# A conditional residual kernel: tile 0 and W's first half issued by two engines, with a new order of tasks

## The chip, the cores and the metric

The kernel runs on 1 core of one Trainium2 chip. The metric is the device time of one execution in microseconds. Before the change the median of 3 runs is 108.7 us (108.12 to 109.39).

## What is computed

```python
def _L0_cond_ref(hidden0, hidden1, x, W, b):
    hidden = jnp.concatenate([hidden0, hidden1], axis=-1)
    x_mean = jnp.mean(x, axis=1, keepdims=True)
    ones_L = jnp.ones((1, L, 1), dtype=x.dtype)
    fused = jnp.concatenate([x, x_mean * ones_L, hidden[:, None, :] * ones_L], axis=-1)
    relation = jax.nn.relu(jnp.einsum('bld,do->blo', fused, W) + b)
    return relation
x = x + _L0_cond_ref(cond_512, cond_512, x, L0_cond_W, L0_cond_b)
```

x is (4, 1024, 512), cond_512 (4, 256), W (1536, 512), b (512), all float32. The first 512 rows of W meet x itself. The next 512 meet the mean of x over a batch row, and the last 512 meet the condition, so those two give one bias vector per batch row. The output is x + relu(x @ W[:512] + bias of the row).

## The kernel before, in words

The 4096 rows of x make 32 **tiles** of 128 rows, 8 to a batch row. A product in float32 is split into high and low parts: a value's `hi` is its float32r rounding and `lo` is the rest, and a tile's result is the sum over four chunks j of 128 columns of hi x w_hi, lo x w_hi and hi x w_lo. That is 12 matmuls for a tile, and 384 for all (the last tile is done in two halves of 256 columns, so it has 24 short ones, and the trace has 396).

x is read twice. Task `Z` loads it in 512-byte rows into one of three `z` buffers, so that VectorE's 32 x 32 transposes (task `T`, L228) give x transposed; ScalarE rounds that to `hi` and sums it for the mean (`h`, L234); VectorE or GpSimd subtracts to get `lo` (`l`, L240). Tiles are taken in **units**: tile 0, tile 1, tiles 2 and 3, and then four at a time. Units are loaded in four quarters of 32 partitions (`Z4.2` is quarter 2 of unit 4). Task `X` loads x a second time, two tiles at once, for the last addition.

W's first 512 rows come in two halves, W0 (chunks j = 0 and 1) and W1 (j = 2 and 3), each in four quarters. `wh` rounds a chunk to w_hi (L204 on ScalarE, L206 on VectorE) and `wl` subtracts to w_lo (L210). `M` loads W's second 512 rows (tile w_mean), `V` the last 512, `C` the condition and `B` b.

**The bias of a batch row r** is a chain in PSUM bank `acc`: ScalarE copies the condition's part there (`as`, L279), VectorE adds four products of w_mean with the row's means (`m`, L284), ScalarE and VectorE fold and split it (`f` L292, `fa` L296, `vh` L300, `vl` L304), one matmul with ones spreads it (`pb`, L308), and ScalarE copies it out (`bc`, L312). The means of row r need all of that row's `h` (`to`, L272 to L275, on GpSimd).

A tile's output leaves PSUM in one of three ways. Tiles 0 to 11 are parked by ScalarE (`K`, L397), then GpSimd adds the bias (`b`, L401), ScalarE takes the relu (`r`, L409) and GpSimd adds x (`F`, L413). Tiles 12 to 17 are parked by VectorE with the bias added (L405). For tiles 18 to 31 ScalarE first puts the bias into the bank (`P`, L384 and L364) and VectorE does relu and addition in one instruction (`F`, L388 and L368). `S` stores a tile. There are five PSUM banks for products; tile t uses bank t mod 5.

**What sets the order** is one table, ORDER (L21 to L49): names of tasks in the order in which they are written, with `@d`, `@a`, `@p` for VectorE, ScalarE and GpSimd (or, for a load, `@a` for ScalarE's DMA queue instead of SyncE's). Each engine does its own tasks strictly in that order, and waits are set by a scheduling layer from the data. DMAs, in the order of the table, take eight completion semaphores in turn, so a DMA waits until the one eight places ahead of it has landed. `fill` is a matmul on zeros (L128) that gives TensorE something to do before the first product.

Before the change `one` is put through a relu (L123), with which ScalarE's function table is loaded, ahead of all tasks. After all tasks, 8 matmuls into `acc` (L427) are issued whose result nobody reads.

Of the kernel before, what the change touches and what calls it, by code (L numbers as in the profile page):

```python
# [18 lines left out]


ORDER = """  # L21
W0.0@a W0.2@a W0.1@a W0.3@a Z0.0 Z0.2 Z0.1 Z0.3 Z1.0 Z1.2 Z1.1 Z1.3 wh0l@d wh0r@a wh1@a W1.0 W1.2 W1.1 W1.3
wl0r@d wl0l@d T0.0 T0.1 h0.0 wl1@d h0.1 l0.0@p fill fill fill fill fill fill fill fill fill fill fill p0.0.0
p0.0.2 Z2.0 Z2.2 Z2.1 Z2.3 p0.1.0 T1.0 l0.1@p T1.1 p0.1.2 h1.0 T0.2 p0.0.1 T0.3 h1.1 p0.1.1 T1.3 p1.0.0 h0.3
l1.0@d p1.0.2 l1.1@d h1.3 l0.3@p p1.1.0 Z3.0 Z3.2 Z3.1 Z3.3 wh3@d h0.2 p1.0.1 p1.1.2 wh2@d l0.2@p p0.3.1 T1.2
p0.3.0 wl3@d l1.3@p p0.2.0 h1.2 p0.2.1 l1.2@p p1.3.0 wl2@d p1.3.2 C p1.2.0 T2.2 V p1.1.1 p0.2.2 T2.0 h2.2 B
p1.2.1 p1.3.1 h2.0 Z4.0 Z4.2 Z4.1 Z4.3 l2.2@d p1.2.2 p0.3.2 T2.3 p2.2 l2.0@d h2.3 p2.0 l2.3@d T2.1 p2.3 h2.1
l2.1@d p3.0 Z5.0 Z5.2 Z5.1 Z5.3 p3.1 T3.3 p2.1 T3.2 h3.3 t2 p3.2 T3.0 h3.2 l3.3@p p3.3 K1@a l3.2@d h3.0 t3
ac0@p t1 p6.2 T3.1 K2@a l3.0@d p4.2 M0 M2 M1 M3 h3.1 t0 p4.3 l3.1@p g0.0 p6.0 K0@a K3@a p6.3 ac1@p p6.1 d0.0
g0.1 p7.0 T4.3 Z6.0 Z6.2 Z6.1 Z6.3 p4.0 T4.1 h4.3 p4.1 T4.0 K6@a l4.3@p T4.2 h4.1 p5.3 h4.2 p7.3 l4.1@p h4.0  # L30
p7.1 K4@a l4.0@d d0.1 p8.3 g1.0 T5.1 p5.2 Z7.0 Z7.2 Z7.1 Z7.3 l4.2@d to0 as0 p5.0 d1.0 T5.3 h5.1 p11.3 T5.2
p5.1 T5.0 l5.1@p p8.2 h5.0 m0.0 p8.1 g1.1 X5.0 m0.1 g2.0 p9.0 d1.1 Z8.0 Z8.2 Z8.1 Z8.3 m0.2 h5.3 p11.0 h5.2
m0.3 l5.3@p p9.3 K5@a l5.0@d p11.2 f0 d2.0 g2.1 p8.0 fa0 p9.2 l5.2@d K8@a d2.1 T6.1 p7.2 vh0 p10.1 vl0 X0.0
K7@a T6.2 p13.3 h6.1 X0.1 T6.3 p10.3 l6.1@p T6.0 pb0 X1.0 p9.1 bc0@a to1 p10.0 as1 b2@p X4.0 K9@a p11.1 m1.0
g3.0 p13.0 b0@p m1.1 Z9.0 Z9.2 Z9.1 Z9.3 h6.3 p10.2 m1.2 g3.1 b1@p p14.0 h6.0 m1.3 p12.0 l6.0@d f1 l6.3@p
p12.1 T7.1 K10@a p12.3 K11@a fa1 b5@p p14.1 T7.0 vh1 X4.1 h7.1 p12.2 vl1 b3@p h6.2 p15.0 T7.3 h7.0 l6.2@d pb1
l7.1@p p14.2 h7.3 T7.2 p16.3 bc1@a l7.0@d h7.2 p13.2 T8.0 as2 to2 p16.2 l7.3@p r0 m2.0 p15.1 r1 m2.1 r2 F0
p14.3 m2.2 p15.3 F1 m2.3 p15.2 K12@d f2 p13.1 d3.0 S1 fa2 p16.0 X5.1 T8.1 S0 vh2 p17.2 b4@p X3.0 h8.0 vl2
p17.1 r5 l8.0@d pb2 F2 p16.1 K13@d bc2@a p17.3 T8.3 P18 F5 p17.0 K14@d r3 h8.1 l7.2@d p18.3 P19 K17@d l8.1@p
p18.2 T8.2 P22 p18.0 T9.0 F3 h8.2 p19.1 r12 l8.2@d p22.3 h9.0 d3.1 T9.1 p22.1 h8.3 T9.2 p18.1 r4 K15@d l8.3@p  # L40
h9.1 p22.2 F18 P20 p19.0 F4 T9.3 P23 p19.3 h9.2 p20.1 S4 K16@d h9.3 S18 p23.1 as3 to3 X2.0 b6@p P21 S2 p23.0
m3.0 S3 p19.2 m3.1 X2.1 b10@p r6 X3.1 p21.3 m3.2 S5 p20.3 X1.1 l9.3@p m3.3 p23.2 l9.2@d f3 p20.2 b7@p fa3
p22.0 F19 vh3 b9@p p20.0 vl3 p21.1 F20 F12 pb3 F22 p21.2 S20 bc3@a X6.1 l9.0@d p21.0 b8@p P27 r7 p23.3 P24
l9.1@p p27.0 F23 P25 p27.2 r8 F21 F6 p27.1 S21 P26 S22 p27.3 F7 S12 p25.2 S6 F27 S19 p25.3 P31r S7 r9 p24.2
X6.0 r10 p31.3r P28 p25.1 F10 r16 p31.2r p31.1r F9 p31.0r S10 p26.2 X7.1 p25.0 b11@p p24.1 F25 p24.0 F8 S25
P30 p26.0 S27 r17 F31r X7.0 r13 p26.1 S8 r11 p28.1 r14 F11 p26.3 p24.3 F26 F17 p28.3 F24 S26 P31l p30.1 S9 F16
P29 S24 p28.2 r15 S17 S11 p30.3 F14 S23 p29.2 S16 F15 p28.0 S14 p30.0 F28 F13 p31.3l S28 p30.2 S31r p29.0 S15
F30 p29.3 S30 p29.1 S13 p31.0l F29 p31.1l p31.2l S29 F31l S31l
""".split()  # L49


# [1 line left out]
def kernel(  # L53
# [66 lines left out]
    nc.vector.memset(one, 1.0)  # L120
# [298 lines left out]
    for name in ORDER:  # L419
# [3 lines left out]
        name, _, engine = name.partition("@")  # L423
        tasks.pop(name)(engine)

    for m, c in ((P, 0), (96, 0), (96, 0), (66, 0), (66, 0), (P, 1), (P, 1), (P, 0)):
        nc.tensor.matmul(acc[:m], lhsT=his[0][:, c : c + m], rhs=w_hi[:, 1], start=True, stop=True)  # L427


# [25 lines left out]
```

## Time and profile before

| | |
|---|---|
| median of 3 runs | 108.7 us |
| the profiled execution, its time | 109.66 us |
| its span, first to last instruction | 107.9 us |
| TensorE busy (PE) | 97.9 us, 91% of the span |
| GpSimd busy (POOL) | 74.8 us, 69% |
| VectorE busy (DVE) | 67.3 us, 62% |
| ScalarE busy (ACT) | 62.0 us, 57% |
| DMA moved | 28.41 MB, mean 263 GB/s |

The profile is one execution. A timeline row gives the start and the busy time in us, the engine, the line and the instruction; behind it in brackets stands how long the engine was idle before it and what ended that. SPq and ACTq are SyncE's and ScalarE's sequencers issuing DMAs; PEld is TensorE loading weights. Matmuls overlap, so the distance of their starts says more than their durations.

### The profile page before, as it was taken

What the parts mean: (1) busy time and instruction counts of PE and PEld (TensorE: products, weight loads), DVE (VectorE), ACT (ScalarE), POOL (GpSimd) and SP (SyncE); (2) the same over time, 40 slices, a digit from 0 to 9 for tenths busy, and PEclk for the clock granted to TensorE, in tenths of its full rate; (3) what the DMA queues carried; (4) which work ended last, traced back from release to release, by engine and by line L of the source; (5) the groups of instructions that cost most, each with busy time, mean ns of one, the idle gap of its engine ahead of it and who ended that gap; (6) DMA issues with size and microseconds to landing.
All of it is one profiled execution on the core that took longest, in us unless ns stands there. A gap on an engine that the chain in (4) does not pass through costs nothing.

```text
span 107.9 us, 1436 instructions
## 1 busy us (share of the span) xinstructions
PE 97.9 (91%) x419; PEld 77.1 (71%) x419; DVE 67.3 (62%) x121; ACT 62.0 (57%) x153; POOL 74.8 (69%) x75
## 2 busy tenths in 40 slices
PE   6913999999999999999999999999999899979960
...
DMA  2878699999999999999999995099999984499995
GB/s 84 186 255 242 167 222 351 249 221 223 231 242 231 221 227 237 226 219 260 387 286 215 258 378 232 21 301 362 343 407 406 374 262 147 178 276 406 403 405 191
DMA packets 27633, 28.41 MB, mean 263 GB/s; under 512 B 1637, under 2 KB 18281, under 8 KB 27626
## 3 DMA queue, kind: packets, MB, share of 16 engines
...
## 4 chain that ended last, share of the span: by engine, by line
DMA 26%; DVE 16%; POOL 15%; ACT 12%; SPq 10%; PE 8%; issue 7%; ACTq 0%; DVEq 0%; POOLq 0%
DMA x<-in_x_dram 13%; SPq L142 10%; DMA w_mean<-in_L_cond_W_dram 8%; POOL x L413 7%; PE po L330 6%; DVE acc L284 5%; ACT hi L234 5%; POOL lo L240 5%; DVE xT L228 3%; DMA z<-in_x_dram 3%; POOL cond L266 2%; DVE w_lo L210 2%; ACT o L409 2%; DMA x<-in_L_cond_W_dram 2%; DVE lo L240 2%
## 5 line engine op out<-in xcount | busy, mean ns | idle before, releaser
L330 PE MATMUL po<-w_hi,hi 128*128 128x512 f32 (+1 forms) x132 | 51.7, 393 | 5.0 <-ACT hi L234 3.9
L330 PE MATMUL po<-w_lo,hi 128*128 128x512 f32 (+1 forms) x132 | 51.1, 388 | 0.0
L330 PE MATMUL po<-w_hi,lo 128*128 128x512 f32 (+1 forms) x132 | 50.7, 387 | 0.0
L330 PEld LDWEIGHTS po<-w_hi,hi 128*128 128x128 f32 x132 | 25.3, 192 | 11.9 <-ACT hi L234 4.8
L240 POOL TENSOR_TENSOR lo<-xT,hi 128x512 fp32r<-128x512 f32 (+1 forms) x20 | 22.2, 1118 | 16.4 <-ACT hi L234 16.4
L330 PEld LDWEIGHTS po<-w_lo,hi 128*128 128x128 f32 x132 | 25.2, 191 | 5.0
L330 PEld LDWEIGHTS po<-w_hi,lo 128*128 128x128 f32 x132 | 25.2, 191 | 5.0
L413 POOL TENSOR_TENSOR x<-o,x 128x512 f32<-128x512 f32 x18 | 22.9, 1295 | 6.8 <-ACT o L409 6.1
L388 DVE SCALAR_TENSOR_TENSOR x<-po,x 128x512 f32<-128x512 f32 x13 | 8.7, 686 | 16.5 <-DMA x<-in_x_dram 8.1
L401 POOL TENSOR_TENSOR o<-o,bias 128x512 f32<-128x512 f32 x12 | 15.3, 1296 | 0.0
L234 ACT ACTIVATE hi<-xT 128x512 fp32r<-128x512 f32 (+2 forms) x24 | 11.9, 498 | 5.1 <-DVE xT L228 5.1
L228 DVE STREAM_TRANSPOSE xT<-z 128x512 f32<-128x512 f32 (+2 forms) x24 | 12.5, 539 | 3.7 <-DMA z<-in_x_dram 2.4
L284 DVE SCALAR_TENSOR_TENSOR acc<-w_mean,tot,acc 128x512 f32<-128x512 f32 x16 | 12.1, 756 | 2.5 <-DMA w_mean<-in_L_cond_W_dram 1.3
L240 DVE TENSOR_TENSOR lo<-px,hi 128x512 fp32r<-128x512 f32 (+1 forms) x16 | 10.3, 642 | 2.2 <-ACT hi L234 2.1
L384 ACT ACTIVATE po<-bias 128x512 f32<-128x512 f32 x13 | 7.5, 589 | 6.8 <-DVE x L388 6.5
L409 ACT ACTIVATE o<-o 128x512 f32<-128x512 f32 x18 | 10.6, 619 | 0.9 <-POOL o L401 0.9
L234 ACT ACTIVATE hi<-px 128x512 fp32r<-128x512 f32 (+1 forms) x16 | 9.0, 560 | 2.6 <-DVE px L228 2.5
L228 DVE STREAM_TRANSPOSE px<-z 128x512 f32<-128x512 f32 (+1 forms) x16 | 10.3, 660 | 0.1
L397 ACT ACTIVATE o<-po 128x512 f32<-128x512 f32 x12 | 6.9, 589 | 0.3 <-PE po L330 0.2
L266 POOL TENSOR_TENSOR cond<-cond,term 128x512 f32<-128x512 f32 x4 | 5.2, 1302 | 1.9 <-ACT term L262 1.9
L262 ACT ACTIVATE term<-wc,cT 128x512 f32<-128x512 f32 x8 | 5.6, 718 | 1.0 <-POOL wc L256 0.9
L128 PE MATMUL acc<-warm 128*128 128x512 bf16 x11 | 4.9, 632 | 1.0 <-DVE one L120 1.0
...
## 6 DMA issues: line engine op xcount, KB each, us to landing
...
out_dram<-x SPq DMA_DIRECT2D x31, 256.0 KB, 3.6
z<-in_x_dram SPq DMA_DIRECT2D x28, 256.0 KB, 8.4
...
w_mean<-in_L_cond_W_dram SPq DMA_DIRECT2D x4, 256.0 KB, 8.5
z<-in_x_dram SPq DMA_DIRECT2D x8, 64.0 KB, 2.5
x<-in_L_cond_W_dram ACTq DMA_DIRECT2D x4, 128.0 KB, 2.8
x<-in_L_cond_W_dram SPq DMA_DIRECT2D x4, 128.0 KB, 3.4
```

The costliest lines, as they stand in the source:

```text
L142: (nc.scalar if e == "a" else nc.sync).dma_start(**kw)
L228: nc.vector.transpose(xT.rearrange("p (n t) -> p n t", t=Q), zs[u % Z_BUFS][:, : n * NQ, j * Q : (j + 1) * Q])
L234: nc.scalar.activation(his[buf][:, col : col + m], xT, AF.Copy, accum_out=sums[:, r, j, s : s + 1])
L240: nc_of[e].tensor_tensor(los[buf][:, col : col + m], xT, his[buf][:, col : col + m].bitcast(F32), ALU.subtract)
L266: nc.gpsimd.tensor_tensor(conds[r % 2], conds[r % 2] if k else b_sb, terms[k], ALU.add)
L284: nc.vector.scalar_tensor_tensor(acc, w_mean[:, j, :], tot[:, r, j : j + 1], acc, ALU.mult, ALU.add)
L330: nc.tensor.matmul(v, lhsT=a[:, col : col + P], rhs=m, start=WAYS[t] != "I" and key not in done, stop=done.count(key) == 3 * J - 1, skip_g ...
L384: nc.scalar.activation(bank(t), biases[r], AF.Copy)
L388: nc.vector.scalar_tensor_tensor(x_tile(t), bank(t), 0.0, x_tile(t), ALU.max, ALU.add)
L401: nc_of[e].tensor_tensor(o, o, biases[r], ALU.add)
L409: nc.scalar.activation(o, o, AF.Relu)
L413: nc.gpsimd.tensor_tensor(x_tile(t), o, x_tile(t), ALU.add)
```

## The change

ORDER is another table. In it, ScalarE's queue issues quarters 2 and 3 of tile 0's z and quarters 2 and 3 of W0, and SyncE's queue the other quarters of these and everything else; before, ScalarE's queue issued all of W0 and nothing else. The relu on `one` becomes a task, placed behind those four issues. There are 12 fills at the start and not 11, and one more fill after the first two tiles. w_hi and w_lo of W0 are made in half chunks that are spread over more engines: `wl0r` goes to GpSimd, and several `wh` and `l` tasks change engines. The 8 matmuls at the end are gone. The rest of the table holds the same tasks in another order.

```diff
 ORDER = """
-W0.0@a W0.2@a W0.1@a W0.3@a Z0.0 Z0.2 Z0.1 Z0.3 Z1.0 Z1.2 Z1.1 Z1.3 wh0l@d wh0r@a wh1@a W1.0 W1.2 W1.1 W1.3
+Z0.2@a Z0.3@a Z0.0 Z0.1 W0.0 W0.1 W0.2@a W0.3@a relu Z1.2 Z1.3 Z1.0 Z1.1 T0.0 W1.2 W1.3 T0.1 h0.0 T0.2 h0.1
...
     nc.vector.memset(sums, 0.0)
-    nc.scalar.activation(one, one, AF.Relu)
     nc.gpsimd.memset(b_sb, 0.0)
...
+    @task("relu")
+    def _(e):
+        nc.scalar.activation(one, one, AF.Relu)
...
-    for m, c in ((P, 0), (96, 0), (96, 0), (66, 0), (66, 0), (P, 1), (P, 1), (P, 0)):
-        nc.tensor.matmul(acc[:m], lhsT=his[0][:, c : c + m], rhs=w_hi[:, 1], start=True, stop=True)
```

What that moves is seen in the built programs. Lines after L123 have other numbers there: L142 of the kernel before is L141 of the changed one, L228 is L231, L284 is L287, and so on.

**ScalarE at the start of the program**, before the change. x_63 is the buffer that takes W's first half, DMAHW1 and DMAHW4 are semaphores of earlier loads:

```order
L123 ACT_TABLE_LOAD
L123 ACTIVATE one<-one 128x1 [waits DVE_49]
L142 DMA x_63<-in_L_cond_W_dram 32x2x512 x2
L142 DMA x_63<-in_L_cond_W_dram 32x2x512 [waits DMAHW1_49]
L142 DMA x_63<-in_L_cond_W_dram 32x2x512 [waits DMAHW4_49]
```

and after it, where z_69 is tile 0's z:

```order
L141 DMA z_69<-in_x_dram 32x4x128 x2
L141 DMA x_63<-in_L_cond_W_dram 32x2x512 x2
L158 ACT_TABLE_LOAD
L158 ACTIVATE one<-one 128x1 [waits DVE_49]
L237 ACTIVATE hi_75,sums<-xT_120 128x128 [waits DVE_49] x2
```

All four loads of the changed kernel stand ahead of the table load and wait for nothing. Before, two of the four quarters of W0 waited for a landing.

**SyncE's loads in the first third of the program**, before. z_69, z_70 and z_71 are the three z buffers, x_64 takes W's last 512 rows:

```order
L142 DMA z_69<-in_x_dram 32x16x128 x4
L142 DMA bias_118<-in_cond_dram 4x256
L142 DMA x_64<-in_L_cond_W_dram 128x2x1024
L142 DMA b_sb<-in_L_cond_b_dram 1x512
L142 DMA z_70<-in_x_dram 32x16x128 x4
L142 DMA z_71<-in_x_dram 32x16x128 x4
L142 DMA w_mean<-in_L_cond_W_dram 32x4x512 x4
L142 DMA z_69<-in_x_dram 32x16x128 x4
```

and after it:

```order
L141 DMA z_69<-in_x_dram 32x16x128 x4
L141 DMA bias_118<-in_cond_dram 4x256
L141 DMA x_64<-in_L_cond_W_dram 128x2x1024
L141 DMA z_70<-in_x_dram 32x16x128 x4
L141 DMA b_sb<-in_L_cond_b_dram 1x512
L141 DMA w_mean<-in_L_cond_W_dram 32x4x512 x4
L141 DMA z_71<-in_x_dram 32x16x128 x4
L141 DMA z_69<-in_x_dram 32x16x128 x4
```

The load of w_mean has gone ahead of unit 5 (the z_71 there); unit 6, the last row, has the same loads ahead of it as before.

**VectorE around the bias chain of batch row 1**, before. The transposes of z_69 are unit 6, those of z_70 unit 7:

```order
L228 STREAM_TRANSPOSE px_142<-z_69 128x512 [waits DVE_49]
L228 STREAM_TRANSPOSE xT_121<-z_69 128x512 [waits Pool_49]
L228 STREAM_TRANSPOSE px_141<-z_69 128x512
L284 SCALAR_TENSOR_TENSOR acc<-w_mean,tot,acc 128x512 [waits DVE_49,Activation_49,Pool_49]
L284 SCALAR_TENSOR_TENSOR acc<-w_mean,tot,acc 128x512 [waits DVE_49] x3
L240 TENSOR_TENSOR lo_91<-px_141,hi_77 128x512 [waits PE_49,Activation_49]
L228 STREAM_TRANSPOSE xT_120<-z_70 128x512 [waits DMAHW5_49,DMAHW6_49,DMAHW4_49,DMAHW3_49]
L296 TENSOR_TENSOR acc<-acc,fold 64x512 [waits Activation_49]
L228 STREAM_TRANSPOSE px_141<-z_70 128x512 [waits DVE_49]
L304 TENSOR_TENSOR v_acc<-acc,v_acc 64x512 [waits PE_49,Activation_49]
```

and after it:

```order
L231 STREAM_TRANSPOSE px_141<-z_69 128x512
L287 SCALAR_TENSOR_TENSOR acc<-w_mean,tot,acc 128x512 [waits Activation_49,Pool_49]
L231 STREAM_TRANSPOSE xT_121<-z_69 128x512
L231 STREAM_TRANSPOSE xT_120<-z_69 128x512 [waits Pool_49]
L287 SCALAR_TENSOR_TENSOR acc<-w_mean,tot,acc 128x512 [waits DVE_49]
L243 TENSOR_TENSOR lo_91<-px_141,hi_77 128x512 [waits PE_49,Activation_49]
L287 SCALAR_TENSOR_TENSOR acc<-w_mean,tot,acc 128x512 [waits DVE_49]
L243 TENSOR_TENSOR lo_93<-px_142,hi_79 128x512 [waits PE_49,Activation_49]
L287 SCALAR_TENSOR_TENSOR acc<-w_mean,tot,acc 128x512 [waits DVE_49]
L231 STREAM_TRANSPOSE px_141<-z_70 128x512 [waits DMAHW5_49,DMAHW6_49,DMAHW4_49,DMAHW3_49]
L231 STREAM_TRANSPOSE xT_121<-z_70 128x512 [waits Pool_49]
L299 TENSOR_TENSOR acc<-acc,fold 64x512 [waits Activation_49]
```

The four additions of row 1's means, which stood together, now have transposes and subtractions of unit 6 between them, and two transposes of unit 7 stand ahead of the fold (L299) instead of one.

More of the change, by code (lines that the diff above doesn't have):

```diff
@@ L21 @@
 ORDER = """
-W0.0@a W0.2@a W0.1@a W0.3@a Z0.0 Z0.2 Z0.1 Z0.3 Z1.0 Z1.2 Z1.1 Z1.3 wh0l@d wh0r@a wh1@a W1.0 W1.2 W1.1 W1.3
[L23 to L46, printed above, removed]
@@ L47 @@
-P29 S24 p28.2 r15 S17 S11 p30.3 F14 S23 p29.2 S16 F15 p28.0 S14 p30.0 F28 F13 p31.3l S28 p30.2 S31r p29.0 S15
-F30 p29.3 S30 p29.1 S13 p31.0l F29 p31.1l p31.2l S29 F31l S31l
+Z0.2@a Z0.3@a Z0.0 Z0.1 W0.0 W0.1 W0.2@a W0.3@a relu Z1.2 Z1.3 Z1.0 Z1.1 T0.0 W1.2 W1.3 T0.1 h0.0 T0.2 h0.1
+l0.0@d wh1l@a wh1r@d W1.0 W1.1 l0.1@p wh0r@d wh0l@a wl1r@d fill fill fill fill fill fill fill fill fill fill
+fill fill p0.1.0 h0.2 wl0r@p wl0l@d p0.0.0 Z2.0 Z2.1 T1.1 p0.0.1 T1.0 wl1l@d p0.1.1 h1.0 Z2.2 Z2.3 T0.3 p0.0.2
@@ new lines @@
+h1.1 T1.2 p0.1.2 T1.3 p1.0.2 l1.1@p h1.2 l1.0@d p1.0.0 Z3.0 Z3.1 p1.1.0 l0.2@p p1.0.1 wh3@a wh2@d p1.1.1
+l1.2@p p1.1.2 Z3.2 Z3.3 wl2@d h1.3 p0.2.1 h0.3 p1.3.0 l1.3@d p1.2.0 l0.3@p p1.2.1 C wl3@d p1.2.2 V p0.2.0
+p1.3.1 Z4.0 Z4.1 p1.3.2 T2.3 p0.3.0 p0.3.1 T2.2 h2.3 p0.2.2 Z4.2 Z4.3 p0.3.2 K1@a l2.3@d T2.0 h2.2 fill p3.3
+T2.1 h2.0 l2.2@p p2.3 h2.1 l2.0@d l2.1@d B p2.2 p3.2 M0 M1 p3.1 T3.0 p3.0 T3.3 h3.0 p2.0 M2 M3 h3.3 l3.0@d
+p2.1 K0@a l3.3@p t2 t1 p6.0 T3.2 K3@a p4.0 T3.1 K2@a ac0@p h3.2 p4.3 h3.1 l3.2@d p7.3 Z5.2 Z5.3 l3.1@p t0 t3
```

19 lines of the change are left out of this document (added).

## The prediction

> **What bounds the kernel now.** I began with the page's first two parts: which engine is full, and when.
>
> ```profile
> PE 97.9 (91%) x419; PEld 77.1 (71%) x419; DVE 67.3 (62%) x121; ACT 62.0 (57%) x153; POOL 74.8 (69%) x75
> PE   6913999999999999999999999999999899979960
> DMA  2878699999999999999999995099999984499995
> ```
>
> TensorE is full from the fifth slice almost to the end; the low ones are the third and fourth, 5 to 11 us into the program. Next, what it waits for:
>
> ```profile
> PE po L330 <- ACT hi L234: 3.9, 1, 3.9
> PE po L330 <- ACT po L384: 0.5, 1, 0.5
> PE po L330 <- ACT po L364: 0.5, 1, 0.5
> ```
>
> One wait of 3.9 us stands ahead of the first product; the next are of 0.5. So the kernel is a stream of 396 products whose start is late, and whose end sets the end of the program. The stream itself, from the timeline of TensorE:
>
> ```profile
> 9.73 0.79 PE L330 MATMUL po<-w_hi,hi 128*128 128x512 f32 x1 [3.89 <-ACT hi L234]
> 11.18 0.63 PE L330 MATMUL po<-w_lo,hi 128*128 128x512 f32 x1
> 12.46 0.63 PE L330 MATMUL po<-w_hi,hi 128*128 128x512 f32 x1
> 15.71 0.39 PE L330 MATMUL po<-w_hi,lo 128*128 128x512 f32 x1
> 17.07 0.39 PE L330 MATMUL po<-w_hi,hi 128*128 128x512 f32 x1
> 102.14 0.28 PE L330 MATMUL po<-w_lo,hi 128*128 128x256 f32 x1
> 102.26 2.02 PE L427 MATMUL acc<-w_hi,hi 128*128 128x512 f32 x8
> ```
>
> Between 11.18 and 12.46 lie three products, 0.427 us each; between 15.71 and 17.07 six, 0.227 us each. TensorE thus starts at half rate and is at full rate well before 15.71. The product at 17.07 is number 25, the first that needs tile 2 or 3. From the last product (102.26) to the end of the span it is 5.6 us: an addition, a store and its landing.
>
> **The start, and what the change does to it.** The issues and what waits for them:
>
> ```profile
> 0.72 4.14 SPq L142 DMA_DIRECT2D z<-in_x_dram  x8
> 0.98 0.86 ACTq L142 DMA_DIRECT2D x<-in_L_cond_W_dram  x2
> 0.97 4.88 PE L128 MATMUL acc<-warm 128*128 128x512 bf16 x11 [0.97 <-DVE one L120]
> 3.78 1.27 ACTq L142 DMA_DIRECT2D x<-in_L_cond_W_dram  x2
> 4.90 1.85 SPq L142 DMA_DIRECT2D x<-in_L_cond_W_dram  x4
> 7.81 0.93 ACT L204 ACTIVATE w_hi<-x 128x256 fp32r<-128x256 f32 x2 [5.60 <-DMA x<-in_L_cond_W_dram]
> z<-in_x_dram SPq DMA_DIRECT2D x8, 64.0 KB, 2.5
> x<-in_L_cond_W_dram ACTq DMA_DIRECT2D x4, 128.0 KB, 2.8
> x<-in_L_cond_W_dram SPq DMA_DIRECT2D x4, 128.0 KB, 3.4
> ```
>
> ScalarE issues two quarters of W0 by 1.84 and then nothing until 3.78: the third waits for a quarter of tile 0's z (in the built order, DMAHW1), the fourth for another. So W0 is whole only at 7.8, and VectorE, which has w_hi and w_lo ahead of tile 0's transposes, brings the first product to 9.73.
>
> In the changed program the first eight loads are tile 0 and W0, four on each queue, and none waits. At 0.43 us an issue (0.86 for two) the last pair is issued from about 2.0. With 2.8 us to landing W0 is whole at 4.9, against 7.8. Tile 0 lands near 3.8 and is transposed and rounded while W0 is under way. The first product then needs half a chunk of w_hi, 0.4 us: 5.4. But 12 fills stand ahead of it, and at 4.88 us for 11 (0.43 apart) they end at 6.1. So the **first product is at 6.1**, 3.6 us sooner.
>
> Not all of that is kept, since after 12 products chunks 2 and 3 are wanted. SyncE issues W1 behind unit 1's four quarters, and those wait for tile 0's landing (3.3 to 3.8); that makes 5.1 to 6.9 where 4.90 to 6.75 was. W1 lands 3.4 us after its last issue began, at 9.9; w_hi takes 0.5 us, so product 13 is at about 10.5. The 12 products before it need 12 x 0.427 = 5.1 us at half rate and 2.7 at full, and have 4.4: they fit or nearly do. Another 12 x 0.227 = 2.7 us later, product 25 can start at 13.3 where it was 17.07: **-3.7 us**. Bounds: -2.0 if W1 is a microsecond later and the stream still slow, -4.0 if W1 is a little sooner. The new fill costs 0.2 and falls into a wait for unit 2. The table load now runs beside transfers; even a microsecond later it holds `h0` and then w_hi, and the wait for W1 covers that.
>
> [...]
>
> **The middle.** Being 3.7 us ahead only helps if every later wait has that much room. The tightest is the bias chain, at the three `pb` matmuls:
>
> ```profile
> 40.27 0.69 DVE L228 STREAM_TRANSPOSE xT<-z 128x512 f32<-128x512 f32 x1
> 43.97 3.13 DVE L284 SCALAR_TENSOR_TENSOR acc<-w_mean,tot,acc 128x512 f32<-128x512 f32 x4 [0.30 <-POOL tot L275]
> 49.55 0.69 DVE L304 TENSOR_TENSOR v_acc<-acc,v_acc 64x512 fp32r<-64x512 f32 x1
> 50.61 0.39 PE L308 MATMUL acc<-v_acc,ones 128*128 128x512 f32 x1
> 58.77 0.39 PE L330 MATMUL po<-w_lo,hi 128*128 128x512 f32 x1
> 59.55 0.50 PE L308 MATMUL acc<-v_acc,ones 128*128 128x512 f32 x1 [0.39 <-DVE v_acc L304]
> ```
>
> For batch row 1 v_acc is done at 50.24 and used at 50.61: 0.37 us of room. For row 2 TensorE waits, and 0.78 us instead of 0.23 lie between two starts. So a stream 3.7 us ahead runs into `pb1` unless that chain comes sooner too. In front of it stand transfers:
>
> ```profile
> 30.28 1.96 SPq L142 DMA_DIRECT2D z<-in_x_dram  x1
> 25.98 9.17 DMA w_mean<-in_L_cond_W_dram
> z<-in_x_dram SPq DMA_DIRECT2D x28, 256.0 KB, 8.4
> ```
>
> w_mean lands at 35.15 before. In the changed order it is ahead of unit 5's 1 MB and should land near 29, so row 0's bias is some 5 us sooner. Unit 6, whose last quarter is issued at 30.28 and with 8.4 us lands near 38.7 to 39.8, has as many bytes ahead of it as before, and the DMA engines are nearly full from slice 6 on; it gains at most the 1 us by which unit 3 can start sooner. And from unit 6's first transpose to v_acc VectorE now has, in order, 8 transposes, 4 additions of means, 2 subtractions, the fold and the split:
>
> ```profile
> L228 DVE STREAM_TRANSPOSE px<-z 128x512 f32<-128x512 f32 x14 | 9.4, 693 | 0.1
> L284 DVE SCALAR_TENSOR_TENSOR acc<-w_mean,tot,acc 128x512 f32<-128x512 f32 x16 | 12.1, 756 | 2.5 <-DMA w_mean<-in_L_cond_W_dram 1.3 <-POOL tot L275 0.8
> L240 DVE TENSOR_TENSOR lo<-px,hi 128x512 fp32r<-128x512 f32 x14 | 9.5, 676 | 1.6 <-ACT hi L234 1.6
> ```
>
> 8 x 0.69 + 4 x 0.76 + 2 x 0.68 + 2 x 0.69 = 11.3 us, less some 0.8 since neighbours overlap a little: 10.5. From a first transpose at 38.8 to 39.9 (40.27 before, as VectorE was busy) v_acc is done at 49.3 to 50.4; I take 49.9. Two more products stand ahead of `pb1` than before, so it would be reached at 48; it **waits about 2 us**, and of the lead 1.0 us is left (0.3 to 1.6). From there to `pb2` the chain (copy of the bias, four additions, fold, split and two parkings) needs about as long as the products between, so row 2's wait of 0.55 is partly kept: lead 1.3. `pb3` has room before and after. **The lead after the middle is 1.2 us** (0.3 to 3.5, the upper end where unit 6 is early and the chain doesn't bind).
>
> **The tail.** Here TensorE waits twice more:
>
> ```profile
> 83.07 0.39 PE L330 MATMUL po<-w_lo,hi 128*128 128x512 f32 x1
> 84.00 0.39 PE L330 MATMUL po<-w_hi,hi 128*128 128x256 f32 x1 [0.55 <-ACT po L364]
> 95.91 0.50 PE L330 MATMUL po<-w_hi,hi 128*128 128x512 f32 x1 [0.55 <-ACT po L384]
> 83.87 7.67 DMA x<-in_x_dram
> 91.63 0.70 DVE x L388
> ```
>
> A bank's new bias waits for the old tile's addition on VectorE, and that for x: 7.67 us for one load at 83.87. Between the starts at 83.07 and 84.00 lie 0.93 us where 0.23 would do, so that wait costs 0.7; the other has the same idle time, which makes 1.4 together. In the changed order x of tiles 24 to 27 is loaded well ahead of their additions, so most of this can go: I take **-1.0** (0 to -1.4; the opposite sign is a rival). The 8 last matmuls start at 102.26 and end at 104.28, inside the 5.6 us of additions and stores: 0. Their cover is the last store; without it they would be 2.0 us.
>
> **Sum.** -1.2 - 1.0 = -2.2 us on the profiled execution, 109.66 (span 107.9) to 107.5. The median of the runs is 0.96 below that execution; the same step from 108.7 gives **106.5 us**. What a measurement can tell from no change is about 1%, 1.1 us.
>
> **Rivals.**
> 1. The bias chain is not in the way (unit 6 lands near 37.5, or VectorE is quicker through it). Then the start's 3.7 less 0.2 for the fill is kept: 108.7 - 3.5 = 105.2. For it: w_mean is sooner by 6 us, and row 0's chain is then out of the way. Against: 11.3 us of VectorE's work in front of `pb1`.
> 2. The chain eats nearly all and the tail keeps its waits: 0.3 to 0.6 gained, 108.2. For it: unit 6 has the same bytes ahead, 0.37 us of room before. Against: row 2's wait and the tail's waits have no reason to stay whole.
> 3. Slower: the last load of x. It now stands 34 product slots (34 x 0.227 = 7.8 us) ahead of the end, behind stores that wait for VectorE's and GpSimd's additions on a queue that goes strictly in order. SyncE waited 13.7 us for GpSimd in seven waits, one of 9.0 us:
>
> ```profile
> SPq L142 <- POOL x L413: 13.7, 7, 9.0
> ```
>
> If it is held 3 us it is issued at 95, lands with 7.67 us at 102.7, and three or four additions (2.2 us), a store's issue and landing (3.4) and 0.8 to the close give a span of 109.1: 1.2 us more than before, 109.9. It decides from an issue at about 94 on.
>
> **How the numbers follow.** My forecast 0.45 (its own range 105.8 to 107.5), rival 1 0.17, rival 2 0.24, rival 3 0.14. Faster by over 1% (below 107.6) is the forecast and rival 1 less a little: 0.61. Within 1%: 0.26. Slower: 0.13. The range 105.0 to 108.9 takes in rivals 1 and 2 and leaves out most of 3.
>
> **What would show it.** First product at about 6.1 and number 25 near 13.3; W0 complete near 5. If W0 is whole only after 7, the first step is wrong. A wait of 1 to 3 us at L308 near 48 to 50 shows the middle right; no wait there, with the start early, shows rival 1. L384 and L364 gone from TensorE's waits show the tail right. Last x load issued after 94 shows rival 3. A stream that is 3 us ahead at 60 and a span as before would put the loss in the tail and make the sum wrong.

## The result: slower by 4%, and the profile after

The changed kernel takes 112.57 us (median, 112.32 to 113.8) against 108.88 for the kernel before on the same chip: 1.040 times as long (1.034 to 1.046). Its profiled execution took 112.71 us with a span of 110.9. The forecast was 106.5 with a range up to 108.9. Here and below a time is the median of all executions of a kernel, while a ratio, with its 95% interval in brackets, compares the faster executions alone with those of the kernel before measured beside them, so that it need not be the quotient of two medians. L308, the bias product, is L311 in the changed kernel, and L304, the lower half of the bias vector, is L307.

The page of the changed kernel, part 2:

```profile
PE   6979999999999599996996999996399999999900
PEclk9999999999999999999999999999958999999995
DMA  2999999999999999999999999999359985999991
GB/s 76 270 233 214 219 252 349 214 224 222 204 209 198 210 206 230 230 256 270 243 211 235 204 344 352 349 328 335 134 185 300 381 341 152 366 381 331 407 341 39
```

The start is nearly as good as hoped: TensorE is busy from the second slice on. But there are now holes in slices 14, 19, 22 and 28 to 29, where the row of before had nines. What they wait for (total us, times, longest):

```profile
PE acc L311 <- DVE v_acc L307: 6.0, 4, 2.6
PE acc L127 <- DVE one L120: 1.0, 1, 1.0
PE po L333 <- ACT w_hi L207: 0.7, 1, 0.7
```

All four bias products wait. On the timeline of TensorE (start, duration, and in brackets the idle time and its releaser):

```profile
6.65 0.80 PE L333 MATMUL po<-w_hi,hi 128*128 128x512 f32 x2 [0.68 <-ACT w_hi L207]
...
13.57 0.58 PE L333 MATMUL po<-w_hi,hi 128*128 128x512 f32 x1
...
37.66 0.50 PE L311 MATMUL acc<-v_acc,ones 128*128 128x512 f32 x1 [1.26 <-DVE v_acc L307]
...
50.84 0.50 PE L311 MATMUL acc<-v_acc,ones 128*128 128x512 f32 x1 [1.08 <-DVE v_acc L307]
...
59.86 0.50 PE L311 MATMUL acc<-v_acc,ones 128*128 128x512 f32 x1 [1.02 <-DVE v_acc L307]
...
79.33 0.50 PE L311 MATMUL acc<-v_acc,ones 128*128 128x512 f32 x1 [2.61 <-DVE v_acc L307]
...
80.97 0.63 PE L333 MATMUL po<-w_lo,hi 128*128 128x512 f32 x1
81.40 0.63 PE L333 MATMUL po<-w_hi,hi 128*128 128x512 f32 x1
```

Product 25 starts at 13.57 instead of 17.07. Then, counted from start to start, 1.65, 1.47, 1.40 and 3.00 us lie in front of the bias products where 0.23 would do: 6.6 us lost, against 0.55 in the kernel before. Behind the fourth, eight products are 0.43 us apart (80.97, 81.40 and on), 1.6 us more; the row PEclk shows a granted clock of 5 and 8 tenths in slices 30 and 31, and the trace one of 0.5 for 3.4 us.

What VectorE does in front of the last two of these waits:

```profile
58.36 0.73 DVE L231 STREAM_TRANSPOSE px<-z 128x512 f32<-128x512 f32 x1 [1.11 <-DMA z<-in_x_dram]
59.12 0.68 DVE L307 TENSOR_TENSOR v_acc<-acc,v_acc 64x512 fp32r<-64x512 f32 x1
...
68.64 1.32 DVE L231 STREAM_TRANSPOSE px<-z 128x512 f32<-128x512 f32 x2 [2.12 <-DMA out_dram<-x]
...
73.14 3.13 DVE L287 SCALAR_TENSOR_TENSOR acc<-w_mean,tot,acc 128x512 f32<-128x512 f32 x4 [1.40 <-POOL tot L278]
...
77.87 0.69 DVE L391 SCALAR_TENSOR_TENSOR x<-po,x 128x512 f32<-128x512 f32 x1 [0.25 <-DMA x<-in_x_dram]
78.59 0.68 DVE L307 TENSOR_TENSOR v_acc<-acc,v_acc 64x512 fp32r<-64x512 f32 x1
```

At 58.36 the first transpose of unit 8 had waited for a load, and the lower half of row 2's bias vector stands right behind it. At 68.64 the same happens with unit 9. Here the page names a store, but the four semaphores on which that transpose waits are those of unit 9's quarters, the last of which landed at 68.42; in the kernel before it landed at 62.67. From there to the fourth bias product one step waits for the next: transposes, means, fold, an addition to x, the split. The same steps in the kernel before, and its bias product, which does not wait:

```profile
63.13 1.30 DVE L228 STREAM_TRANSPOSE px<-z 128x512 f32<-128x512 f32 x2
...
70.25 3.13 DVE L284 SCALAR_TENSOR_TENSOR acc<-w_mean,tot,acc 128x512 f32<-128x512 f32 x4 [0.45 <-POOL tot L275]
...
75.39 0.68 DVE L304 TENSOR_TENSOR v_acc<-acc,v_acc 64x512 fp32r<-64x512 f32 x1
```

```profile
76.24 0.39 PE L308 MATMUL acc<-v_acc,ones 128*128 128x512 f32 x1
```

So the loads came later. They carry the same 28.41 MB, but from the 11th to the 15th slice the core moves 204, 209, 198, 210, 206 GB/s. In the kernel before, the same row reads:

```profile
GB/s 84 186 255 242 167 222 351 249 221 223 231 242 231 221 227 237 226 219 260 387 286 215 258 378 232 21 301 362 343 407 406 374 262 147 178 276 406 403 405 191
```

231, 242, 231, 221, 227, a mean of 230 against 205. And a quarter of z takes longer from issue to landing, 9.4 us where it was 8.4:

```profile
z<-in_x_dram SPq DMA_DIRECT2D x28, 256.0 KB, 9.4
```

By the trace's records of packets, a packet of 512 bytes (all of z: 16,384 of them) took 46.4 ns on the mean, against 41.8. Why should the same packets be slower? One thing that the prediction passed over in the new order: the kernel before takes the four quarters of a unit as 0, 2, 1, 3, so that neighbours in the queue go to different halves of the 128 partitions (quarter i fills partitions 32i to 32i + 31). The change takes them 0, 1, 2, 3 or 2, 3, 0, 1. That is theory A. Theory B puts the loss on the new places of the tasks (the mean part of W ahead of unit 5, loads of x between the halves of units 8 and 9, other work ahead of the bias vector on VectorE); theory C on the start or the missing last matmuls.

### The profile page after: what moved, and what is told of

It reads as the page before. It is cut to its first block, busy times and chain, and to the rows that moved or that the text cites. A ratio compares the mean times of both kernels' runs of the same rounds, so it can differ in the third digit from the quotient of the medians.

```text
span 110.9 us, 1434 instructions
## 1 busy us (share of the span) xinstructions
PE 97.6 (88%) x413; PEld 75.7 (68%) x413; DVE 67.8 (61%) x121; ACT 62.9 (57%) x154; POOL 75.2 (68%) x76
## 2 busy tenths in 40 slices
DMA packets 27633, 28.41 MB, mean 256 GB/s; under 512 B 1637, under 2 KB 18281, under 8 KB 27626
## 4 chain that ended last, share of the span: by engine, by line
DMA 35%; PE 24%; SPq 12%; DVE 9%; POOL 7%; ACT 4%; issue 3%; ACTq 1%; DVEq 0%; POOLq 0%
DMA x<-in_x_dram 25%; PE po L333 23%; SPq L141 12%; DMA b_sb<-in_L_cond_b_dram 7%; DMA x<-in_L_cond_W_dram 4%; DVE acc L287 3%; POOL cond L269 2%; DVE w_lo L213 2%; POOL o L404 2%; ACT o L412 2%; ACTq L141 1%; POOL x L416 1%; DVE w_hi L209 1%; DVE xT L231 1%; DVE acc L299 1%
## 5 line engine op out<-in xcount | busy, mean ns | idle before, releaser
L333 PE MATMUL po<-w_hi,hi 128*128 128x512 f32 (+1 forms) x132 | 51.0, 390 | 0.7 <-ACT w_hi L207 0.7
L243 POOL TENSOR_TENSOR lo<-xT,hi 128x512 fp32r<-128x512 f32 (+2 forms) x20 | 21.8, 1101 | 14.5 <-ACT hi L237 14.5
L404 POOL TENSOR_TENSOR o<-o,bias 128x512 f32<-128x512 f32 x12 | 15.3, 1292 | 0.0
L231 DVE STREAM_TRANSPOSE px<-z 128x512 f32<-128x512 f32 (+1 forms) x16 | 10.4, 673 | 7.5 <-DMA z<-in_x_dram 5.4
L231 DVE STREAM_TRANSPOSE xT<-z 128x512 f32<-128x512 f32 (+2 forms) x24 | 12.0, 527 | 4.0 <-DMA z<-in_x_dram 3.9
L287 DVE SCALAR_TENSOR_TENSOR acc<-w_mean,tot,acc 128x512 f32<-128x512 f32 x16 | 12.0, 749 | 3.2 <-ACT o L400 1.5
L387 ACT ACTIVATE po<-bias 128x512 f32<-128x512 f32 x13 | 7.6, 594 | 8.0 <-DVE x L391 7.3
L400 ACT ACTIVATE o<-po 128x512 f32<-128x512 f32 x12 | 6.6, 587 | 1.8 <-PE po L333 1.8
L311 PE MATMUL acc<-v_acc,ones 128*128 128x512 f32 x4 | 2.0, 497 | 6.0 <-DVE v_acc L307 6.0
L127 PE MATMUL acc<-warm 128*128 128x512 bf16 x13 | 5.4, 587 | 1.0 <-DVE one L120 1.0
```

What stands on the lines that cost most here:

```text
L231: nc.vector.transpose(xT.rearrange("p (n t) -> p n t", t=Q), zs[u % Z_BUFS][:, : n * NQ, j * Q : (j + 1) * Q])
L243: nc_of[e].tensor_tensor(los[buf][:, col : col + m], xT, his[buf][:, col : col + m].bitcast(F32), ALU.subtract)
L287: nc.vector.scalar_tensor_tensor(acc, w_mean[:, j, :], tot[:, r, j : j + 1], acc, ALU.mult, ALU.add)
L333: nc.tensor.matmul(v, lhsT=a[:, col : col + P], rhs=m, start=WAYS[t] != "I" and key not in done, stop=done.count(key) == 3 * J - 1, skip_g ...
L387: nc.scalar.activation(bank(t), biases[r], AF.Copy)
L400: nc.scalar.activation(o, bank(t), AF.Copy)
```

## The experiments

**E1: the change with alternating quarters.** For units 2 to 9 and the mean part of W, in the same places of the order:

```diff
-M0 M1 ... M2 M3 ... Z5.2 Z5.3 ... Z5.0 Z5.1
+M0 M2 ... M1 M3 ... Z5.0 Z5.2 ... Z5.1 Z5.3
```

> The changed kernel with the quarters of every load of z from unit 2 on, and of the mean part of W, taken 0, 2, 1, 3 in the same places, as the kernel before takes them; nothing else differs from the changed kernel. Theory A (two neighbouring quarters on one queue are slower than two taken from the two halves of the partitions): the stretch from the landing of unit 7 to that of unit 9 falls from 22.5 us to about 18 (17.9 in the kernel before), the waits of the four bias products on TensorE fall from 6.6 us together to about 2.5, the half-rate stretch after the fourth goes, and the time is 107 to 108.5 us. Theory B (the rate is not the cause; the places of the tasks are): 112 to 113 us, stretch 22 us, the waits as they are. Theory C (the start with two queues or the missing last matmuls cost time by themselves): 112 to 113 us.

Measured: 106.78 us, 0.977 of the kernel before (0.964 to 0.990). One permutation of equal loads turns 4% slower into 2% faster. (The execution that was profiled is one of its longer ones, 108.47.) Its page and its timeline of VectorE:

```profile
GB/s 79 259 229 221 247 234 319 179 235 251 235 219 227 227 238 239 226 279 264 244 229 251 242 315 403 401 404 283 124 236 276 393 358 158 368 386 250 406 402 114
```

```profile
64.76 1.32 DVE L231 STREAM_TRANSPOSE px<-z 128x512 f32<-128x512 f32 x2 [0.39 <-DMA z<-in_x_dram]
...
69.26 3.13 DVE L287 SCALAR_TENSOR_TENSOR acc<-w_mean,tot,acc 128x512 f32<-128x512 f32 x4 [1.40 <-POOL tot L278]
...
74.72 0.69 DVE L307 TENSOR_TENSOR v_acc<-acc,v_acc 64x512 fp32r<-64x512 f32 x1
```

```profile
PE acc L311 <- DVE v_acc L307: 1.7, 3, 0.6
```

Slices 11 to 15 are back at a mean of 229 GB/s, a 512-byte packet takes 42.1 ns, unit 9's transposes and everything behind them come 3.9 us sooner, and the bias products wait 1.7 us in place of 6.0. The half-rate stretch is gone as well (PEclk reads 9 in every slice but the last). (The stretch from unit 7 to unit 9 became 20.4 us by the ends of their packets, 22.6 in the change and 18.0 before, not the 18 expected; that the loads of x still stand between the halves may be why.) Theories B and C said 112 to 113.

**E2: the kernel before with neighbouring quarters**, the counterpart:

```diff
-Z5.0 Z5.2 Z5.1 Z5.3 ... M0 M2 M1 M3
+Z5.0 Z5.1 Z5.2 Z5.3 ... M0 M1 M2 M3
```

> The kernel before with the quarters of z from unit 2 on, and of the mean part of W, taken 0, 1, 2, 3 in the same places. Theory A: the stretch from unit 7 to unit 9 grows from 17.9 us to about 21 or 22, units 8 and 9 land 3 to 4 us later, TensorE waits at the bias products of rows 2 and 3, and the time is 110.5 to 112.5 us. Theory B and theory C: 108.5 to 109.3 us, the same stretch as before.

Measured: 109.6 us, 1.013 (1.001 to 1.025). The loads slow down as theory A has it (packet 43.7 ns, unit 9's last packet at 64.5 and not 61.7), but the time only by 0.9 us, not by 2 to 4: the only bias product that waits does so no longer than before.

```profile
z<-in_x_dram SPq DMA_DIRECT2D x28, 256.0 KB, 9.2
```

```profile
PE acc L308 <- DVE v_acc L304: 0.4, 1, 0.4
```

The kernel before had room for slow loads, since TensorE itself ran 3.5 us later; E12 below, with an early start in front of the same middle, bears that out. My expectation forgot it.

**E3: the kernel before without its last eight matmuls**, and **E4: the change with the lower half of the bias vector (`vl`) sooner on VectorE.**

```diff
-    for m, c in ((P, 0), (96, 0), (96, 0), (66, 0), (66, 0), (P, 1), (P, 1), (P, 0)):
-        nc.tensor.matmul(acc[:m], lhsT=his[0][:, c : c + m], rhs=w_hi[:, 1], start=True, stop=True)
```

```diff
-vh0 T5.3 p10.1 X0.0 T5.2 h5.3 p9.3 vl0 ... T8.0 vh2 p14.1 g3.0 F2 vl2 ... F22 vh3 b10@p p23.2 S22 vl3
+vh0 vl0 T5.3 p10.1 X0.0 T5.2 h5.3 p9.3 ... vh2 vl2 T8.0 p14.1 g3.0 F2 ... vh3 vl3 F22 b10@p p23.2 S22
```

> The kernel before without the eight matmuls into the accumulator bank at the end, nothing else. They write what nobody reads. Theories A and B: 108.5 to 109.3 us, no difference that can be measured. Theory C: 110 us or more.

> The changed kernel with the lower half of the bias vector, for rows 0, 2 and 3, placed on VectorE right behind its upper half and ahead of the transposes of units 5 and 8 and of the last step of tile 22, for which it stood in line. Theory A: the landings stay late (22.5 us from unit 7 to unit 9), the bias products wait about 1.4 us less in row 0, 1.2 less in row 2 and 0.7 less in row 3, and since the fourth still waits over 2 us the time is 109.5 to 111.5 us. Theory B: the waits of the four bias products fall from 6.6 us together to about 2.5, and the time is 107 to 108.5 us. Theory C: 112 to 113 us, since the waits only come up elsewhere.

E3 took 108.78 beside 108.73 for the kernel before (1.007, 1.000 to 1.014): by this interval the missing matmuls cost 1.4% at most, so that half of theory C falls; the other half, the start, falls with E1, which has the same start. E4 took 111.74, 1.030 (1.019 to 1.040), far from theory B's 107 to 108.5, and between the 109.5 to 111.5 of theory A and the 112 to 113 of theory C.

```profile
51.09 0.70 PE L311 MATMUL acc<-v_acc,ones 128*128 128x512 f32 x1 [1.97 <-DVE v_acc L307]
...
78.26 0.50 PE L311 MATMUL acc<-v_acc,ones 128*128 128x512 f32 x1 [1.01 <-DVE v_acc L307]
```

The waits of rows 0 and 2 are gone, but row 1 now waits 1.97 us in place of 1.08: what the first wait no longer takes, the next one does. Behind this wait, too, TensorE runs at half rate for a while, 0.43 us from start to start where 0.23 is the full rate, with a PEclk of 8 and 5 tenths in slices 19 and 20:

```profile
51.59 0.63 PE L333 MATMUL po<-w_hi,hi 128*128 128x512 f32 x1
52.02 0.63 PE L333 MATMUL po<-w_hi,lo 128*128 128x512 f32 x1
```

**E5 and E6: source or destination?** Neighbouring quarters differ in two ways from alternating ones: they are written to the same half of the partitions, and they are read from neighbouring 512-byte pieces of the same rows. Both programs put quarter 1 on partitions 64 to 95 and quarter 2 on 32 to 63, for z, W and the mean part of W alike (the sums over partitions don't mind). E5 is the change with this map, E6 is E1 with it. (The map also holds for tiles 0 and 1 and for W's first half, whose order E1 left as in the change.)

```diff
+    PQ = [0, 2, 1, 3]
-                dma(e, out=z[i * Q : (i + 1) * Q, : n * NQ], ...)
+                dma(e, out=z[PQ[i] * Q : (PQ[i] + 1) * Q, : n * NQ], ...)
```

> The changed kernel with its quarters still read 0, 1, 2, 3 from memory, but quarter 1 is put on partitions 64 to 95 and quarter 2 on 32 to 63, for z, W and the mean part of W alike; the sums over the partitions are the same in another order. Theory A1 (the destination: two loads into the same half of the partitions one behind the other are slow): as the alternating order, the mean 512-byte packet falls from 46.4 ns to about 42, unit 9 lands near 63.5 and not 67.4, and the time is 106 to 108 us. Theory A2 (the source: reading neighbouring columns of the same rows back to back is slow): 46 ns, 112 to 113 us.

> The counterpart: the changed kernel with its quarters read 0, 2, 1, 3 from memory, with quarter 2 put on partitions 32 to 63 and quarter 1 on 64 to 95, so that the loads go to the partitions in their plain order. Theory A1 (destination): 46 ns for a 512-byte packet, unit 9 near 67 us, time 111 to 113 us. Theory A2 (source): 42 ns, 106 to 108 us.

| kernel | read | written to halves | 512-byte packet, ns | unit 9's last packet, us | time, us | ratio (interval) |
|---|---|---|---|---|---|---|
| the change | neighbours | same | 46.4 | 67.4 | 112.57 | 1.040 (1.034 to 1.046) |
| E6 | apart | same | 45.3 | 66.1 | 111.28 | 1.027 (1.016 to 1.038) |
| E5 | neighbours | alternating | 42.4 | 62.5 | 109.56 | 1.013 (1.000 to 1.026) |
| E1 | apart | alternating | 42.1 | 63.5 | 106.78 | 0.977 (0.964 to 0.990) |

The issue-to-landing rows of E5 and E6 lean the same way (the column also holds the time that a load stands behind others: in E11 below it is 7.2 to 7.5 us where a quarter lands every 1.2 us or so; E1 has 9.0; so the packets are the better measure):

```profile
z<-in_x_dram SPq DMA_DIRECT2D x28, 256.0 KB, 8.7
```

```profile
z<-in_x_dram SPq DMA_DIRECT2D x28, 256.0 KB, 9.2
```

The rate of the loads goes with the destination: 3 to 4 ns of a packet, against 0.3 to 1.1 for the source. E4 and E10 (below), which load as the change does, have 45.3 and 45.5 ns, so a difference of 1 ns between two executions shows nothing. Nor are 4 ns the rule: E2 lies 1.9 above the kernel before (43.7 against 41.8), and E12 1.3 above E8 (45.0 against 43.7).

The time follows less cleanly. E5's four executions took 108.0 to 110.33, and whether it is slower than the kernel before is open. Its stream of products is the earliest of all (last product at 98.73), but its span ends 7.5 us later, 5.7 in the change; so E5 missed the 106 to 108 expected. E1 has 7.0 there, and E7, further on, 7.6; E8 and E9, which have the end of the kernel before, have 5.2. In E1 the last load of x is issued at 93.45 and seven stores stand behind it in the queue:

```profile
93.45 0.45 SPq L141 DMA_DIRECT2D x<-in_x_dram  x1
93.94 5.36 SPq L141 DMA_DIRECT2D out_dram<-x  x7
```

The chain of work that ended last, followed back from the end, is in the change TensorE's products up to 105.49. In E5, and in E7 below, it goes through that last load of x and the additions behind it:

```profile
93.32 5.55 DMA x<-in_x_dram
```

```profile
93.38 5.93 DMA x<-in_x_dram
```

In E1 it goes through a store (`out_dram`) from 94.68 to 99.63, and its last load of x landed at 99.36. So with TensorE ahead, the transfers at the end of the change's order set the end; that was read from the chain, and no run moves that load.

**E7: E1 with E4's edit.**

> The changed kernel with the alternating order of quarters and with the lower half of the bias vector ahead of the transposes in rows 0, 2 and 3. With the alternating order alone TensorE still waited 0.8, 0.8, 0 and 0.6 us at the four bias products. Theory A: rows 0 and 3 lose 1.2 us of that, and the time falls by 0.5 to 1 us against the alternating order alone, to 105.5 to 106.5 us, if the loads of x and the stores at the end do not take it back. Rival (the end is set by the transfers, since the last product came 5.5 us earlier with the alternating order and the span fell by 4.2 only): no difference from the alternating order alone, 106.3 to 107.2 us.

Measured: 107.56 us, 0.989 (0.984 to 0.993). No gain over E1 is shown; the rival is right that there is none, and its number (106.3 to 107.2) is a little low. The chain shown above fits it.

**E8: the start alone.** The change's order up to the 16th product, alternating quarters, then the order of the kernel before.

```diff
 ... p1.2.0 l0.3@p p1.2.1 C wl3@d
-p1.2.2 V p0.2.0 p1.3.1 Z4.0 Z4.1 ... M0 M1 ... M2 M3 ... Z5.2 Z5.3
+p0.3.1 p0.3.0 p0.2.0 p1.3.2 T2.2 V ... B ... Z4.0 Z4.2 Z4.1 Z4.3 ... Z5.0 ... M0 M2 M1 M3
```

> The changed kernel's order up to the last step on W (the lower part of its fourth block, behind the 16th product), with quarters of z alternating, and from there everything in the order of the kernel before, so also its place of the mean part of W, behind unit 5. It says what the start is worth if the middle is left as it was. If the prediction's first step is right and the middle was what ate it, TensorE leads by 3 to 3.5 us at the 25th product and the time is 105.5 to 107 us. If the lead can't be kept because the middle of the kernel before has no room either (its mean part of W lands behind unit 5 whenever the start ends), 108 to 109 us.

Measured: 106.76 us, 0.983 (0.974 to 0.993), in the range of the first reading; the profiled execution took 106.61. Product 25 is at 13.68, and the last one at 99.57, where it was 102.14 in the kernel before: 2.6 of the 3.4 us are kept, with nothing of the change's middle. TensorE's largest waits:

```profile
PE po L333 <- ACT o L400: 1.3, 1, 1.3
...
PE acc L311 <- DVE v_acc L307: 0.5, 1, 0.5
```

**E9: E8 with two lower parts of unit 5 ahead of the mean part of W.**

```diff
-m0.0 p8.1 g1.1 X5.0 m0.1 ... m0.2 h5.3 p11.0 h5.2 m0.3 ... l5.0@d ... l5.2@d
+l5.0@d h5.2 l5.2@d m0.0 p8.1 g1.1 X5.0 m0.1 ... m0.2 h5.3 p11.0 m0.3
```

> The order of the start-only kernel (the change up to the 16th product, the kernel before from there, quarters alternating), with two lower parts of unit 5 (l5.0 and l5.2, with the upper part h5.2) taken ahead of the first step on the mean part of W. There VectorE sat from 32.45 to 34.18 us waiting for the mean part of W with l5.0 and l5.2 behind it, and TensorE lost 1.5 us at the product of 39.22. Expected: that gap goes; the wait at the third bias product (0.6 us lost) grows by part of it, since that chain does not start earlier; time 105 to 106.3 us against 106.8 of the start-only kernel. Rival (the third bias product takes all of it): 106.3 to 107 us.

Measured: 107.47 us, 0.989 (0.980 to 0.997), above both readings. The gap stayed (1.83 us from start to start, 1.72 in E8). I had taken the VectorE work that ended nearest to 39.22 for the releaser. The row above names another, ScalarE's copy of a finished bank (L400). In E8 it ended at 39.17 and stood behind the fold of row 0's bias, which waited for the means:

```profile
37.34 0.59 ACT L295 ACTIVATE fold<-acc 64x512 f32<-64x512 f32 x1 [1.27 <-DVE acc L287]
...
38.57 0.60 ACT L400 ACTIVATE o<-po 128x512 f32<-128x512 f32 x1
...
39.22 0.50 PE L333 MATMUL po<-w_hi,hi 128*128 128x512 f32 x1 [1.33 <-ACT o L400]
```

The edit moved work that TensorE did not wait for.

**E10: the change with the first three bias products six matmuls later.**

```diff
-pb0 ... p9.0 ... p10.0 bc0@a | pb1 p12.3 to2 bc1@a b1@p p13.1 | pb2 h8.0 p17.3 F5 T8.2 S2 bc2@a S1 p16.0
+p9.0 ... p10.0 pb0 bc0@a | p12.3 to2 b1@p p13.1 pb1 bc1@a | h8.0 p17.3 F5 T8.2 S2 S1 p16.0 pb2 bc2@a
```

> The changed kernel with the bias products of rows 0, 1 and 2 each six matmuls (two groups of three, 1.36 us) later on TensorE, and the copies that read them behind them; quarters as in the change. Theory A (the slow loads decide through the fourth bias product, whose chain starts from the landing of unit 9 at 68.4): the first three waits of 1.4, 1.2 and 1.2 us go, TensorE is up to 3.8 us ahead at product 270, and then waits that much longer at the fourth, which stays near 79.3 us; time 111.5 to 113 us, and the half-rate stretch stays. Rival (each of the four waits adds its part to the end): 108 to 109.5 us.

Measured: 111.56 us, 1.026 (1.015 to 1.037), as theory A has it. The profiled execution, the quickest, took 110.05.

```profile
PE acc L311 <- DVE v_acc L307: 3.3, 2, 3.1
```

Of the three early waits 0.2 us is left, TensorE is at product 271 2.1 us sooner than in the change, and the fourth bias product waits 3.1 us in place of 2.6. It starts at 77.69 and not 79.33, since the loads were quicker in this execution (45.5 ns a packet, unit 9's last at 65.7). So the four waits don't add up to the end; the slow chain behind unit 9 sets it. The half rate did not come back (products 0.23 us apart behind the wait, PEclk 9 in every slice but the last), though the wait was longer. The four executions of the change, with mean clocks of 0.967, 0.971, 0.987 and 0.988, took 112.44, 112.71, 112.32 and 113.8: those with the higher clock are not the shorter ones, so the half rate is not what made the change slow.

**E11: the loads by themselves.** Four stretches of 16 quarters on one queue, from the same 4 MB, in one execution:

```diff
+    phases = [("aa", (0, 1, 2, 3), (0, 1, 2, 3)), ("bb", (0, 2, 1, 3), (0, 2, 1, 3)),
+              ("ab", (0, 1, 2, 3), (0, 2, 1, 3)), ("ba", (0, 2, 1, 3), (0, 1, 2, 3))]
+            for s, d in zip(src, dst):
+                nc.sync.dma_start(out=zs[name, u][d * Q : (d + 1) * Q], in_=zv[u // 2, s, ...])
```

> Loads alone, no computation (the output is left out but for 256 KB): four stretches of 16 quarter loads of 256 KB, all issued by SyncE one behind the other, from the same 4 MB of x into four sets of buffers: (1) quarters and partitions 0, 1, 2, 3; (2) both 0, 2, 1, 3; (3) quarters read 0, 1, 2, 3, put on partition quarters 0, 2, 1, 3; (4) read 0, 2, 1, 3, put on 0, 1, 2, 3. Theory A1 (destination): stretches 1 and 4 take 10 to 20 per cent longer than 2 and 3, some 1.3 us a quarter against 1.15. Theory A2 (source): 1 and 3 are the slow ones. If the difference needs the other engines' traffic on the same memory: all four alike, 1.1 to 1.2 us a quarter.

The issues on SyncE (the first 16 take 15.3 us; from the second stretch on they go at the pace of the transfers, 16 in 18.8 to 19.4 us, and a load lands 7.2 to 7.5 us behind its issue), and the rate in 40 slices of 2.06 us:

```profile
16.12 18.98 SPq L46 DMA_DIRECT2D bb<-in_x_dram  x16
35.15 18.78 SPq L46 DMA_DIRECT2D ab<-in_x_dram  x16
53.97 19.35 SPq L46 DMA_DIRECT2D ba<-in_x_dram  x16
```

```profile
GB/s 18 252 214 210 211 214 208 215 215 214 216 225 225 217 224 226 224 219 224 225 224 218 224 225 224 219 224 226 225 208 215 215 214 216 212 210 215 212 27 127
```

The packets of `aa` run from 1.8 to 21.3 us and those of `ba` from 58.9 to 78.9; between lie `bb` and `ab`. The row shows it as steps: about 213, then 223, then 213 GB/s. The two stretches with alternating destinations are alike, whatever is read; the other two are 4 to 5% slower, and their quarters land in pairs (after 1.3 and after 1.15 us) where the others come every 1.17. That is A1, though less than the 10 to 20% expected. The packets say the same: 46.2 ns in `ba` against 44.4 in `bb` and 44.3 in `ab`. (`aa` has 44.6 over all, since its first four quarters have 38.8; the other twelve have 46.2 to 47.0.) That is 4% alone; beside the rest of the kernel the four pairs of programs (46.4 and 42.1, 45.3 and 42.4, 43.7 and 41.8, 45.0 and 43.7 ns) differ by 3 to 10%.

No run shows by what mechanism the half of the partitions counts. The gain of alternating is small alone, 4 to 5%, and in the kernel the order of quarters decided the sign of the result (E1: 0.977 of the kernel before, the change 1.040).

**E12: E8 with neighbouring quarters.**

> The start-only kernel (the change up to the 16th product, the order of the kernel before from there) with the quarters of z from unit 2 on and of the mean part of W taken 0, 1, 2, 3 as the change takes them. It is the fourth corner of a square: the change's start with the change's middle took 112.6 us with neighbouring quarters and 106.8 with alternating ones, and with the middle of the kernel before 106.8 with alternating ones. If slow loads eat the lead whatever the middle (the kernel before lost only 0.9 us to them because it was late on TensorE anyway): 110.5 to 112.5 us. If it is the change's middle order that has no room for slow loads, as the mean part of W ahead of unit 5 and the loads of x between the halves of units 8 and 9 leave less: 107.3 to 109 us.

Measured: 110.26 us beside 109.2 for the kernel before. The four executions took 108.91, 109.04, 111.48 and 113.34, too far apart to decide by the time; the lower two lie at the upper end of the second reading. The profiled execution is the first, and its stream shows more. Start of a product on TensorE, us (the four bias products are counted with the others):

| product | before | change | E1 | E8 | E12 |
|---|---|---|---|---|---|
| 25 | 17.07 | 13.57 | 13.36 | 13.68 | 13.89 |
| 171 | 50.16 | 48.46 | 48.46 | 48.72 | 50.12 |
| 211 | 59.89 | 60.20 | 58.54 | 58.53 | 59.88 |
| 271 | 73.52 | 73.84 | 72.16 | 72.15 | 73.52 |
| 291 | 78.08 | 81.82 | 77.42 | 76.70 | 78.41 |
| 391 | 100.96 | 104.12 | 98.64 | 98.39 | 101.13 |

With neighbouring quarters E12 has lost the whole lead of 3.2 us by product 171 (E8 keeps 1.4), and at other places than the change (a bank, not a bias product; the wait of the second row is at 85.12):

```profile
PE po L333 <- ACT o L400: 2.1, 2, 1.9
PE po L333 <- ACT po L367: 1.3, 1, 1.3
```

So slow loads eat the lead in either middle: 2.7 us of stream at product 391 (E12 less E8), and 5.5 us in the change (the change less E1). That does not show the change's middle to have less room. Of the 5.5 us, 1.6 are the half rate, and the other 3.9 are as much as unit 9 landed later (68.42 against 64.54); in E12 it landed 2.6 us later than in E8 (64.30 against 61.66). The loads themselves were slowed more in the change, by 4.3 ns a packet against 1.3, and why stays open. With quick loads the two middles take the same time (E1 and E8, 106.78 and 106.76). So theory B is not borne out as a cause of the slower time.

## Why the prediction was wrong

- **The start** was right: product 25 at 13.57 (13.3 predicted), 3.5 us sooner. W0 was whole at 6.0 and not 4.9, so that the first product waited for w_hi and not for the fills, and came at 6.65, not 6.1. The order of tasks changed along with the queues, and no run parts the two.
- **The middle failed**, in two sentences. That unit 6 "has as many bytes ahead of it as before" and "gains at most the 1 us" took each load at the speed of before; unit 6 landed at 40.57, not 38.7 to 39.8, and a packet of z took 46.4 ns, not 41.8, over the whole stream. At unit 6 the speed was worth little (39.97 in E1). And "`pb3` has room before and after" was not worked out from a row: the wait there was the largest, 2.6 us, since unit 9 landed 5.75 us later. Of these E1 takes back 3.9 by the order of quarters alone; the other 1.9 stay in E1, which has the change's start and its places of the tasks. For `pb1` the step was about right (1.2 us lost, 2 predicted); the wait at `pb0`, where the split stood behind transposes of unit 5 (E4), was not foreseen either. Lead after the middle: 1.2 us predicted, 0.3 us behind at product 211 and 3.7 behind at product 291.
- **The tail** had the right sign: the waits on L384 and L364 (now L387 and L367) are gone from the page. From product 331 (5.3 us behind) to 391 (3.2 behind) the change gained 2.1 us on the kernel before.
- **The eight matmuls** gave nothing that E3 could show when they were left out, as predicted.
- **Rivals 1 and 2** did not come about. **Rival 3** named slower, by another mechanism: its condition came true (the last load of x issued at 97.17), but the stream was 3 us late by then, and the end was TensorE's. Where the stream is early its mechanism is there: in E5 and E7 the chain ends through that load, issued at 93.3.
- With the destinations alternating as before, the sum holds: in E1 the lead is 1.35 us at product 211 (1.2 predicted), grows by 1.7 us in the tail (from 0.66 at product 291 to 2.32 at 391; 1.0 predicted), and the time is 106.78 (106.5 predicted). That the total fits so well is in part luck: between products 211 and 291 0.7 us of the lead go that the sum keeps, the tail gives 0.7 more than the sum has, and the end is 1.2 us longer; and the execution in which this was read took 108.47. The step that failed is thus the silent one that an order of equal loads does not change their speed.
- Two sums in the prediction are off by 0.1 without effect: 2.0 + 2.8 is 4.8, and 34 x 0.227 is 7.7. The last product starts at 102.14; 102.26 is the first of the eight matmuls behind it.
